# Summed neighbour layers of a graph network: steps between TensorE's results and VectorE's use of them, one PSUM bank per kind of group, inputs asked for a group ahead

## The chip, the cores and the metric

The kernel runs on one core of a Trainium2 chip. Its metric is the device time of one execution in microseconds (us); the median of three runs stands for the kernel before. TensorE (PE) does matrix products, VectorE (DVE) and ScalarE (ACT) work on elements, GpSimd (POOL) gathers rows, SyncE (SP) issues most of the transfers. L12 is line 12 of the kernel; L81, L85 and L90 lie in small helpers for VectorE's operations on two tensors, on a tensor and scalars, and on both.

## What is computed

A graph of 6250 nodes with 128 features and 100,000 edges, sorted by their target, goes through four blocks. Each block is `x = x + layer(relu(layernorm(x)))`:

```python
# block 0: mean over the incoming edges, one layer
agg = segment_sum(h[src], dst) / max(count, 1)
x = x + relu(h @ W_self.T + agg @ W_neigh.T + bias)
# block 1: a filter for each edge from its length, a product over the incoming edges
bf  = ssp(ssp(exp(coeff * (dist - centers)**2) @ W1 + b1) @ W2 + b2)
agg = segment_prod(h[src] * edge_attr * bf * cut, dst)
x = x + ssp(agg @ W3 + b3)
# block 2: three layers of the mean, relu between them
for i in range(3):
    h = relu_but_last(mean(h[src] by dst) @ W_agg[i] + h @ W_root[i] + b[i])
x = x + h
# block 3: three attention layers with batch norm
```

The change touches blocks 0 and 2, and one load of block 1.

## The kernel before

The nodes are cut into 50 tiles of 125. **A mean is formed in two ways.** For the first 38 tiles, in ten groups (`GROUPS`: nine of four tiles, one of two), it is a matrix product: an adjacency of small counts in eight-bit floats, 6250 sources by 500 targets for a group, is the moving operand, and the node rows, split into three bfloat16 parts whose sum is the float32 value, are the weights. One group takes 50 x 3 = 150 matmuls of 500 columns into one PSUM bank `o` (`product_steps`, from L1085). For the last 12 tiles, three groups of four (`LATE`), GpSimd gathers the source row of each edge, VectorE adds along the edges (195 columns in batches of five, L90), the running sums go to DRAM, and the rows at each target's last edge are fetched back; TensorE turns them (`late_sums`, from L901).

Then a group's **node terms** follow, the same for both kinds (`node_terms`, from L1097): the group's own rows, transposed, are loaded from DRAM; two matmuls make y, own rows by one matrix and the mean by the other (L1106, L1107); ScalarE adds the bias (`out_t`, L1108); TensorE turns y back (L1112); a function `rows` that the caller gives adds it to x or norms it on VectorE and ScalarE (`norm_in_two`, from L1070). All this goes through the PSUM tiles named `nt`, two of them, one bank each.

**The order is written out by hand.** These functions are generators; a `yield` marks a point at which other work may be put. Afterwards `chain` (L1149) binds every instruction of TensorE, VectorE and ScalarE to its predecessor on the same engine, so that each engine runs in just the written order. SP and GpSimd are not bound in that way, but their queues also run in order.

- *Block 0* (its `nodes_of` from L1250) still has to build the adjacencies. A step of `build_adj` (L1015) is eight one-hot rows on VectorE (L85; tiles `hot_p`, `hot_n`, three buffers each), four matmuls that count into `cnt` (L1029) and one conversion on ScalarE (L1030). A group of four has 25 steps, one of two 13. At each step stand six matmuls of the product of the group before, every second step a piece of node terms of the group before that (`follow`), and a piece of late sums (`late_`). At the end of a group's products comes the mean, `agg`, on VectorE, as the last act of `product_steps`.
- *Block 2* (`woven`, L1115; its `nodes_of` from L1319) streams the same adjacencies back from DRAM, one unit per layer and group, 30 in all. A unit has 15 slots of ten products; in slots 1, 3, 5, 7 and 9 stands a piece of node terms of the group before, in each slot a piece of late sums, and in most a piece of work for block 3 (`beside`). `Stream` (L1162) keeps `BUFS` pieces of five source tiles loaded or being loaded.
- *Block 1* (`filter_in_order`) takes blocks of sixteen columns of edges; `inputs` (L662) loads their lengths (`dist`, 1 MB, two buffers) when a block begins, and edge attributes (`ea`) and gathered rows in smaller blocks.

Of the kernel before, what the change touches and what calls it, by code (L numbers as in the profile page):

```python
# [20 lines left out]
P = 125  # L21
# [26 lines left out]
def kernel(ctx: ExitStack, tc: tile.TileContext, a: dict, out: bass.AP):  # L48
# [583 lines left out]
    def filter_in_order(table, hist, src_all, wp, pool, ps, tails):  # L632
# [28 lines left out]

        def inputs(i):  # L662
            c0 = i * HB
            if c0 % DB == 0:
                dist = pool.tile([128, DB, P], F32, name="dist", bufs=2)
                nc.sync.dma_start(dist.rearrange("p c q -> p (c q)"), bass.AP(
                    tensor=ew_dram.tensor, offset=ew_dram.offset + c0 * P, ap=[[0, 128], [1, DB * P]]))
                st["dist"] = dist
# [138 lines left out]
    def turn_rows(ht, t0, h, pool, ps):  # L807
# [3 lines left out]
        for k0, k1 in ((0, 3), (3, NW)):  # L811
            tp = ps.tile([128, 4, 128], F32, name="nt", bufs=2)
# [88 lines left out]
    def late_sums(su, table, nodes_of, pace, pool, ps):  # L901
# [9 lines left out]
        for _ in range(5):  # L911
            yield
# [18 lines left out]
        carry = ps.tile([128, NW - 1, 128], F32, name="nt", bufs=2)[:, 0, :]  # L931
# [7 lines left out]
        given = []  # L939
# [5 lines left out]
        for _ in range(4):  # L945
            yield
        for (t0, t1), rows in zip(LATE, given):
            inv = load_inv(t0, t1, pool, "_late")
            tp = ps.tile([128, NW - 1, 128], F32, name="nt", bufs=2).rearrange("f k p -> f (k p)")
            for j in range(t1 - t0):  # L950
                transpose(tp[:, j * P:(j + 1) * P], rows[:P, j, :])
            agg = pool.tile([128, NC], F32, name="agg_late", bufs=1)
            tt(agg, tp[:, :NC], inv, OP.mult)
            yield
            yield from nodes_of(t0, t1, [agg], "_late")
# [129 lines left out]
    def product_steps(parts, adj, t0, t1, agg, pool, ps):  # L1085

        n = (t1 - t0) * P
        inv = load_inv(t0, t1, pool)
# [5 lines left out]
        agg.append(pool.tile([128, NC], F32, name="agg", bufs=1))  # L1094
        tt(agg[0][:, :n], o[:, :n], inv[:, :n], OP.mult)

    def node_terms(ht, t0, t1, agg, w_agg, w_self, bias, func, rows, pool, ps, of):  # L1097
# [3 lines left out]
        own = pool.tile([128, NC], F32, name="own" + of, bufs=1)  # L1101
        nc.sync.dma_start(own[:, :n], ht[:, t0 * P:t1 * P])
        yield
        out_t = pool.tile([128, NC], F32, name="out_t" + of, bufs=1)
        y = ps.tile([128, NW - 1, 128], F32, name="nt", bufs=2).rearrange("f k p -> f (k p)")[:, :n]
        nc.tensor.matmul(y, lhsT=w_self, rhs=own[:, :n], start=True, stop=False)  # L1106
        nc.tensor.matmul(y, lhsT=w_agg, rhs=agg[0][:, :n], start=False, stop=True)  # L1107
# [7 lines left out]
    def woven(units, beside):  # L1115
# [5 lines left out]
        while ahead:  # L1121
            steps, look, then, sums = ahead
            ahead = None
            for at in range(15):
# [4 lines left out]
                if at in (1, 3, 5, 7, 9):  # L1129
                    next(follow, None)  # L1130
# [1365 lines left out]
```

## Time and profile before

| what | us |
|---|---|
| median of three runs | 5659.31 |
| lowest and highest run | 5656.65, 5667.72 |
| the profiled execution | 5665.26 |
| its span, first to last instruction | 5663.2 |

The mean clock granted to TensorE over the span is 0.863 of full speed. The shares of the span, and the stretch of each part, with what fills it:

```profile
PE 4650.4 (82%) x27333; PEld 3229.0 (57%) x27333; DVE 4038.3 (71%) x12698; ACT 3319.3 (59%) x6907; POOL 3033.6 (54%) x3016
```

| stretch, us | what |
|---|---|
| 0 to 317 | first norm, constants, index tables |
| 317 to 917 | block 0's sums |
| 930 to 2028 | block 1's filter |
| 2028 to 2207 | block 1's ends, hand-over |
| 2207 to 3263 | block 2's three layers |
| 3270 to 5663 | block 3's three attention layers |

PEld is the loading of weights, which overlaps the products. In a row of stretches the first two numbers are its bounds and its length; then come the busy time and, in brackets, the instructions of PE, PEld, DVE, ACT and POOL, the granted clock of TensorE (1.00 is full speed), the share of the 16 DMA engines and the rate in GB/s. In a row of waits stand the engine, what it was about to do with its line, after the arrow the engine and line that released it, then the total of us, how often, and the longest. Waiting costs nothing by itself; it matters on the engine that has no time to spare in that stretch.

### The profile page before, as it was taken

To read this page: it belongs to the slowest core of one execution; us is meant where nothing else is said; L and a number is where in the kernel's file an instruction comes from. 1 tells how busy PE (TensorE), PEld (TensorE's weight loads), DVE (VectorE), ACT (ScalarE), POOL (GpSimd) and SP (SyncE) were. 2 spreads that over 40 slices of the span, in tenths; PEclk is the share of its full clock that TensorE was granted. 3 is DMA by queue.
4 is the path that set the end of the run, shared out by engine and by line. 5 is a ranking of instruction groups with operands and counts; after the bars stand their busy time and mean duration, and the time that the engine had idled before them with its cause. 6 is when DMAs were issued, how large, how long until landed. Compare 5 with 4: busy or idle time off the path is not lost. (4 is left out here: it accounts for less than half of the span.)

```text
span 5663.2 us, 88527 instructions
## 1 busy us (share of the span) xinstructions
PE 4650.4 (82%) x27333; PEld 3229.0 (57%) x27333; DVE 4038.3 (71%) x12698; ACT 3319.3 (59%) x6907; POOL 3033.6 (54%) x3016
## 2 busy tenths in 40 slices
PE   3368886889888857989999959999779999599997
PEld 3224443444444433444444448888668889488886
DVE  7988773999999954766667557776377774577763
ACT  0155453999999954333333346667566668466675
POOL 0155203777777733747647347774157761377750
PEclk9999896655565568999999979999889999799998
DMA  1244324666666645889989656675466663576652
GB/s 46 51 146 148 116 81 117 194 197 198 189 197 196 190 135 153 274 289 331 321 282 327 219 188 198 193 200 154 137 175 196 195 189 96 171 200 194 197 160 83
DMA packets 574066, 1036.46 MB, mean 183 GB/s; under 512 B 113872, under 2 KB 320271, under 8 KB 571283
## 3 DMA queue, kind: packets, MB, share of 16 engines
q1 hardware_dynamic: 470888, 829.77, 45.6%
q0 software_dynamic: 96864, 198.00, 14.4%
q8 instruction: 217, 3.56, 0.3%
q10 hardware_dynamic: 5828, 2.94, 0.2%
q14 instruction: 269, 2.20, 0.1%
HBM read 690.23 MB, written 340.10 MB: 182 GB/s over the span
## 5 line engine op out<-in xcount | busy, mean ns | idle before, releaser
L63 POOL DMA_INDIRECT rows<-gtable,l_src x1200 | 1226.4, 1022 | 566.0 <-issue 328.6
L1895 PE MATMUL o<-m,hst 125*128 125x160 f32 x6000 | 943.3, 310 | 154.0 <-ACT m L2064 154.0
L1895 PEld LDWEIGHTS o<-m,hst 125*128 125x128 f32 x6000 | 902.4, 198 | 196.5 <-ACT m L2064 177.3
L63 POOL DMA_INDIRECT s_rows<-table,s_src x780 | 759.6, 974 | 429.8 <-issue 198.0
L63 POOL DMA_INDIRECT rows<-table,src_all x800 | 817.3, 1022 | 256.6 <-issue 212.7
L2059 PE MATMUL cnt<-hot_n,hot_c 128*125 128x250 f32 x3840 | 932.0, 386 | 8.0 <-ACT hot_c L1886 4.9
L1092 PEld LDWEIGHTS <-parts 128*128 128x128 bf16 x5040 | 503.6, 100 | 521.4 <-issue 57.6
L1092 PE MATMUL o<-piece,parts 128*128 128x500 fp8e4 (+1 forms) x3540 | 758.2, 373 | 7.2 <-ACT parts L1059 5.4
L2059 PEld LDWEIGHTS cnt<-hot_n,hot_c 128*125 128x125 f32 x3840 | 701.9, 192 | 84.4 <-ACT hot_c L1886 5.8
L1886 ACT ACTIVATE hot_c<-hot,coef_t 128x125 f32<-128x125 bf16 x1920 | 698.4, 389 | 0.1
L2064 ACT ACTIVATE m<-cnt 125x1000 f32<-125x1000 f32 x480 | 473.3, 986 | 29.8 <-PE cnt L2059 29.5
L693 PE MATMUL z<-w,s 128*125 128x128 f32 x1600 | 366.0, 399 | 113.4 <-DVE s L90 113.1
L90 DVE SCALAR_TENSOR_TENSOR acc<-acc,ex,rows 125x130 f32<-125x130 f32 x1197 | 424.1, 354 | 35.6
L693 PEld LDWEIGHTS z<-w,s 128*125 128x125 f32 x1600 | 313.2, 290 | 219.4 <-DVE s L90 180.3
L1030 ACT ACTIVATE adj<-cnt 128x1000 fp8e4<-128x1000 f32 x238 | 289.8, 1217 | 225.1 <-PE cnt L1029 224.6
L684 PE MATMUL z<-bf,w 128*128 128x500 f32 x400 | 369.9, 1025 | 31.4 <-ACT bf L653 27.3
L1885 ACT ACTIVATE hot_n<-half_n 128x250 f32<-128x250 bf16 x960 | 382.9, 399 | 1.9 <-DMA half_n<-node 1.6
L1092 PE MATMUL o<-adj,parts 128*128 128x500 fp8e4 (+1 forms) x1500 | 355.2, 378 | 0.0
L85 DVE TENSOR_SCALAR hot_n<-l_slot,l_id_t 128x250 f32<-128x250 f32 x960 | 301.2, 357 | 71.5 <-PE cnt L2059 47.4
L1205 ACT ACTIVATE over<-piece,few 128x1250 bf16<-128x1250 fp8e4 (+1 forms) x200 | 256.1, 1281 | 141.4 <-issue 124.7
L90 DVE SCALAR_TENSOR_TENSOR s_acc<-s_acc,s_same,s_rows 128x128 f32<-128x128 f32 x776 | 272.9, 352 | 31.1 <-DMA sum_hist<-s_acc 5.8
L653 ACT ACTIVATE soft<-soft,half 128x500 f32<-128x500 f32 (+1 forms) x400 | 286.7, 717 | 13.0
(574 smaller groups left out, 7266.8 us busy)
## 6 DMA issues: line engine op xcount, KB each, us to landing
piece<-adj SPq DMA_DIRECT2D x270, 312.5 KB
late_hist<-acc SPq DMA_DIRECT2D x150, 455.0 KB
hot<-hot SPq DMA_DIRECT2D x240, 256.0 KB
half_n<-node SPq DMA_DIRECT2D x480, 125.0 KB
dist<-ew_dram SPq DMA_DIRECT2D x50, 1000.0 KB
sum_hist<-s_acc SPq DMA_DIRECT2D x156, 320.0 KB
hot_t<-hot_t SPq DMA_DIRECT2D x192, 256.0 KB
ea<-in_edge_attr SPq DMA_DIRECT2D x100, 448.0 KB
```

The lines of the kernel that those rows point to most:

```text
L63: nc.gpsimd.indirect_dma_start(out=dst, out_offset=None, in_=table, in_offset=bass.IndirectOffsetOnAxis(ap=idx, axis=0))
L85: nc.vector.tensor_scalar(o, x, s1, None, op0=op0)
L90: nc.vector.scalar_tensor_tensor(o, x, s, y, op0=op0, op1=op1)
L684: nc.tensor.matmul(z1, lhsT=w1, rhs=bf, start=False, stop=True)
L693: nc.tensor.matmul(z2[:, j, :], lhsT=s1[:, j, :], rhs=w2, start=False, stop=j == HB - 1)
L1030: nc.scalar.activation(adj[:, :, NW * (w - w0):NW * (w - w0 + k)].rearrange("p l (w k) -> p w l k", k=NW), cnt[:, :k, :T * NW].rearrange(" ...
L1092: yield nc.tensor.matmul(o[:, :n], lhsT=parts.columns(l, 1, s)[:, 0, :], rhs=adj(l), start=(l == 0 and s == 0), stop=(l == T - 1 and s == 2))
L1885: nc.scalar.activation(hot_n[:, w, :], half_n[:, w // 2, :], AF.Copy)
L1886: nc.scalar.activation(hot_c[:, w, :P], lt.hot[:, w0 % WB + w, :P], AF.Copy, scale=coef_t[g][:, w0 + w:w0 + w + 1])
L1895: nc.tensor.matmul(o, lhsT=hst[:, l, :D], rhs=m[:P, l, :], start=(l == 0), stop=(l == T - 1))
L2059: nc.tensor.matmul(cnt[:P, w, :T * NW], lhsT=hot_c[:, w, :P], rhs=hot_n[:, w, :], start=True, stop=True)
L2064: nc.scalar.activation(m[:P, :, :, u * 4:u * 4 + 4].rearrange("p l k q -> p k l q"), cnt[:P, :, :T * NW].rearrange("p w (k l) -> p k l w", ...
```

## The change

Six things are done, all of them to the order of instructions and to buffers; the arithmetic is the same.

1. The mean is no longer taken at the end of a group's products. `product_steps` hands back a function, which `node_terms` calls as its first step, in the next group.
2. `node_terms` gets more steps: one more after y, and `gap` steps between the transposes and VectorE's use of them (four in block 0, one in block 2); ordinary groups of block 0 begin four steps later. In exchange a piece is taken at every step in block 0, not at every second, and in nine slots of a unit in block 2, not in five.
3. `late_sums` waits `lead` steps ahead of the first batch (eight in block 0; ten, five, five in block 2; it was five), seven steps in place of four ahead of the late groups, and `gap` between their transposes and the mean.
4. The two `nt` banks become one `nt` for ordinary groups and one `nt_late` for late ones.
5. Own rows are loaded by `load_own` as soon as a group's products begin (for late groups a group ahead), into two buffers.
6. In block 1 the lengths of a block are asked for one block ahead, into three buffers; `BUFS` goes from 12 to 11.

```diff
@@ -659,13 +659,18 @@
             act(l, l, AF.Ln, bias=half[:o.shape[0]], scale=0.5)
             stt(o, z, 0.0, l, OP.max, OP.add)
 
+        def distances(c0):
+            dist = pool.tile([128, DB, P], F32, name="dist", bufs=3)
+            nc.sync.dma_start(dist.rearrange("p c q -> p (c q)"), bass.AP(
+                tensor=ew_dram.tensor, offset=ew_dram.offset + c0 * P, ap=[[0, 128], [1, DB * P]]))
+            return dist
+
         def inputs(i):
             c0 = i * HB
             if c0 % DB == 0:
-                dist = pool.tile([128, DB, P], F32, name="dist", bufs=2)
-                nc.sync.dma_start(dist.rearrange("p c q -> p (c q)"), bass.AP(
-                    tensor=ew_dram.tensor, offset=ew_dram.offset + c0 * P, ap=[[0, 128], [1, DB * P]]))
-                st["dist"] = dist
+                st["dist"] = st.pop("dist_ahead", None) or distances(c0)
+                if c0 + DB < C:
+                    st["dist_ahead"] = distances(c0 + DB)
             if c0 % NB == 0:
                 rows = pool.tile([128, NB, D], F32, name="rows", bufs=4)
                 ea = pool.tile([P, NB, D], F32, name="ea", bufs=4)
@@ -808,8 +813,8 @@
 
         on_pe = []
         h_t = pool.tile([128, NW, P], F32, name="h_turned", bufs=1)
-        for k0, k1 in ((0, 3), (3, NW)):
-            tp = ps.tile([128, 4, 128], F32, name="nt", bufs=2)
+        for k0, k1, of in ((0, 3, ""), (3, NW, "_late")):
+            tp = ps.tile([128, 4, 128], F32, name="nt" + of, bufs=1)
             on_pe += [nc.tensor.transpose(tp[:, k - k0, :P], h[:, k, :], ident[:P, :P]) for k in range(k0, k1)]
             nc.scalar.activation(h_t[:, k0:k1, :], tp[:, :k1 - k0, :P], AF.Copy)
         nc.sync.dma_start(ht[:, t0 * P:(t0 + NW) * P], h_t.rearrange("f k p -> f (k p)"))
@@ -898,7 +903,13 @@
 
     SB = 5
 
-    def late_sums(su, table, nodes_of, pace, pool, ps):
+    def load_own(ht, t0, t1, pool, of=""):
+        own = pool.tile([128, NC], F32, name="own" + of)
+        nc.sync.dma_start(own[:, :(t1 - t0) * P], ht[:, t0 * P:t1 * P])
+        return own
+
+    def late_sums(su, table, ht, nodes_of, pool, ps, lead, pace, gap):
+
 
 
         def rows_of(c0):
@@ -908,7 +919,7 @@
             return rows
 
         given, prev = [rows_of(0), rows_of(SB)], None
-        for _ in range(5):
+        for _ in range(lead):
             yield
         for b, c0 in enumerate(range(0, C3, SB)):
             if c0 + 2 * SB < C3:
@@ -928,7 +939,7 @@
         fixed = pool.tile([128, D], F32, name="s_fixed", bufs=1)
         nc.gpsimd.memset(fixed, 0.0)
         gather_some(fixed, sum_hist, su.fix, 128 * C3)
-        carry = ps.tile([128, NW - 1, 128], F32, name="nt", bufs=2)[:, 0, :]
+        carry = ps.tile([128, NW - 1, 128], F32, name="nt_late", bufs=1)[:, 0, :]
         nc.tensor.matmul(carry, lhsT=su.flow, rhs=prev, start=True, stop=True)
         held = pool.tile([128, D], F32, name="s_held", bufs=1)
         nc.scalar.activation(held, carry, AF.Copy)
@@ -936,23 +947,27 @@
             yield
         tt(fixed, held, fixed, OP.add)
         scatter(sum_hist, su.fix, fixed, 128 * C3)
-        given = []
+        given, own = [], [None, load_own(ht, *LATE[0], pool, "_late")]
         for t0, t1 in LATE:
             rows = pool.tile([128, SB, D], F32, name="s_rows", bufs=4)
             for j in range(t1 - t0):
                 gather(rows[:, j, :], sum_hist, su.end[:, t0 - TE + j:t0 - TE + j + 1])
             given.append(rows)
-        for _ in range(4):
+        for _ in range(7):
             yield
         for (t0, t1), rows in zip(LATE, given):
-            inv = load_inv(t0, t1, pool, "_late")
-            tp = ps.tile([128, NW - 1, 128], F32, name="nt", bufs=2).rearrange("f k p -> f (k p)")
+            own, inv = own[1:], load_inv(t0, t1, pool, "_late")
+            if t1 < T:
+                own.append(load_own(ht, t1, t1 + 4, pool, "_late"))
+            tp = ps.tile([128, NW - 1, 128], F32, name="nt_late", bufs=1).rearrange("f k p -> f (k p)")
             for j in range(t1 - t0):
                 transpose(tp[:, j * P:(j + 1) * P], rows[:P, j, :])
+            for _ in range(gap):
+                yield
             agg = pool.tile([128, NC], F32, name="agg_late", bufs=1)
             tt(agg, tp[:, :NC], inv, OP.mult)
             yield
-            yield from nodes_of(t0, t1, [agg], "_late")
+            yield from nodes_of(t0, t1, [own[0], lambda agg=agg: agg], "_late")
 
 
 
@@ -1082,34 +1097,43 @@
             ts(h[:, j, :], x[:, j, :], mv[:, j, 0:1], OP.subtract, rstd[:, j:j + 1], OP.mult)
         nc.scalar.activation(h, h, AF.Relu)
 
-    def product_steps(parts, adj, t0, t1, agg, pool, ps):
+    def product_steps(parts, adj, ht, t0, t1, agg, pool, ps):
 
         n = (t1 - t0) * P
+        agg.append(load_own(ht, t0, t1, pool))
         inv = load_inv(t0, t1, pool)
         o = ps.tile([128, NC], F32, name="o", bufs=2)
         for l in range(T):
             for s in range(3):
                 yield nc.tensor.matmul(o[:, :n], lhsT=parts.columns(l, 1, s)[:, 0, :], rhs=adj(l),
                                        start=(l == 0 and s == 0), stop=(l == T - 1 and s == 2))
-        agg.append(pool.tile([128, NC], F32, name="agg", bufs=1))
-        tt(agg[0][:, :n], o[:, :n], inv[:, :n], OP.mult)
-
-    def node_terms(ht, t0, t1, agg, w_agg, w_self, bias, func, rows, pool, ps, of):
+
+        def mean():
+            m = pool.tile([128, NC], F32, name="agg", bufs=1)
+            tt(m[:, :n], o[:, :n], inv[:, :n], OP.mult)
+            return m
+
+        agg.append(mean)
+
+    def node_terms(t0, t1, agg, w_agg, w_self, bias, func, rows, pool, ps, of, gap):
 
 
         n = (t1 - t0) * P
-        own = pool.tile([128, NC], F32, name="own" + of, bufs=1)
-        nc.sync.dma_start(own[:, :n], ht[:, t0 * P:t1 * P])
+        own, mean = agg
+        mean = mean()
         yield
         out_t = pool.tile([128, NC], F32, name="out_t" + of, bufs=1)
-        y = ps.tile([128, NW - 1, 128], F32, name="nt", bufs=2).rearrange("f k p -> f (k p)")[:, :n]
+        y = ps.tile([128, NW - 1, 128], F32, name="nt" + of, bufs=1).rearrange("f k p -> f (k p)")[:, :n]
         nc.tensor.matmul(y, lhsT=w_self, rhs=own[:, :n], start=True, stop=False)
-        nc.tensor.matmul(y, lhsT=w_agg, rhs=agg[0][:, :n], start=False, stop=True)
+        nc.tensor.matmul(y, lhsT=w_agg, rhs=mean[:, :n], start=False, stop=True)
         nc.scalar.activation(out_t[:, :n], y, func, bias=bias, scale=1.0)
         yield
-        r = ps.tile([128, NW - 1, 128], F32, name="nt", bufs=2)[:P, :t1 - t0, :]
+        yield
+        r = ps.tile([128, NW - 1, 128], F32, name="nt" + of, bufs=1)[:P, :t1 - t0, :]
         for k in range(t1 - t0):
             nc.tensor.transpose(r[:, k, :], out_t[:, k * P:(k + 1) * P], ident)
+        for _ in range(gap):
+            yield
         rows(r, out_t[:, :n])
 
     def woven(units, beside):
@@ -1126,7 +1150,7 @@
                     pass
                 if at == 0:
                     ahead = next(units, None)
-                if at in (1, 3, 5, 7, 9):
+                if at in (0, 1, 2, 3, 4, 5, 6, 8, 9):
                     next(follow, None)
                 if sums and at == (10 if late else 0):
                     for _ in late or ():
@@ -1163,7 +1187,7 @@
 
 
 
-        L, BUFS = 5, 12
+        L, BUFS = 5, 11
 
         def __init__(self, pool):
             self.pool, self.tiles, self.at, self.seen = pool, {}, -1, 0
@@ -1253,7 +1277,10 @@
                     def rows(y, _):
                         stt(x, y, 0.0, x, OP.max, OP.add)
 
-                    yield from node_terms(ht_dram[0], t0, t1, agg, w_n, w_s, bias, AF.Identity, rows, pool, ps, of)
+                    if not of:
+                        for _ in range(4):
+                            yield
+                    yield from node_terms(t0, t1, agg, w_n, w_s, bias, AF.Identity, rows, pool, ps, of, 4)
                     bulk(turned(x_after[0], t0, t1 - t0), x)
                     h_n = pool.tile([P, NW - 1, D], F32, name="h_n" + of, bufs=1)[:, :t1 - t0, :]
                     yield from norm_in_two(h_n, x, t1 - t0)
@@ -1263,7 +1290,7 @@
 
                 traced = nc.cur_bb.bb.instructions
                 n0 = len(traced)
-                late_ = late_sums(su, table[0], nodes_of, 3.6, pool, ps)
+                late_ = late_sums(su, table[0], ht_dram[0], nodes_of, pool, ps, 8, 3.6, 4)
                 before, follow, then = iter(()), iter(()), iter(())
                 for t0, t1 in GROUPS:
                     n = (t1 - t0) * P
@@ -1271,14 +1298,13 @@
                     for step, _ in enumerate(build_adj(t0, t1, flat, pool, ps, hi_t, id_t, slots_b)):
                         for _ in islice(before, 6 if t1 - t0 == 4 else 12):
                             pass
-                        if step % 2:
-                            next(follow, None)
+                        next(follow, None)
                         next(late_, None)
                     for piece in (before, follow):
                         for _ in piece:
                             pass
                     agg = []
-                    before = product_steps(parts, lambda l, flat=flat, n=n: flat[:, l * n:(l + 1) * n], t0, t1, agg, pool, ps)
+                    before = product_steps(parts, lambda l, flat=flat, n=n: flat[:, l * n:(l + 1) * n], ht_dram[0], t0, t1, agg, pool, ps)
                     follow, then = then, nodes_of(t0, t1, agg)
                 for piece in (before, follow, then, late_):
                     for _ in piece:
@@ -1326,18 +1352,19 @@
                         nc.sync.dma_start(ht_dram[2 + i][:, t0 * P:t1 * P], y_t)
                         split(parts[i + 1], t0, n, h, pool)
 
-                    yield from node_terms(ht_dram[1 + i], t0, t1, agg, w_a[i], w_r[i], bias[i], AF.Relu, rows, pool, ps, of)
+                    yield from node_terms(t0, t1, agg, w_a[i], w_r[i], bias[i], AF.Relu, rows, pool, ps, of, 1)
                     yield
                     return
                 x = pool.tile([P, NW - 1, D], F32, name="h_g" + of, bufs=1)[:, :n, :]
                 bulk(x, turned(x_after[1], t0, n))
-                yield from node_terms(ht_dram[3], t0, t1, agg, w_a[i], w_r[i], bias[i], AF.Identity, lambda y, _: tt(
-                    x, y, x, OP.add), pool, ps, of)
+                yield from node_terms(t0, t1, agg, w_a[i], w_r[i], bias[i], AF.Identity, lambda y, _: tt(
+                    x, y, x, OP.add), pool, ps, of, 1)
                 bulk(turned(x_dram, t0, n), x)
                 h = pool.tile([P, NW - 1, D], F32, name="h_g3" + of, bufs=1)[:, :n, :]
                 yield from norm_in_two(h, x, n)
                 yield
-                tp = ps.tile([128, NW - 1, 128], F32, name="nt", bufs=2).rearrange("f k p -> f (k p)")[:, :n * P]
+                yield
+                tp = ps.tile([128, NW - 1, 128], F32, name="nt" + of, bufs=1).rearrange("f k p -> f (k p)")[:, :n * P]
                 for k in range(n):
                     nc.tensor.transpose(tp[:, k * P:(k + 1) * P], h[:, k, :], ident[:P, :P])
                 p0, p1 = t0 * P // T, t1 * P // T
@@ -1349,7 +1376,7 @@
                 for i in range(3):
                     for g, (t0, t1) in enumerate(GROUPS):
                         agg = []
-                        steps = product_steps(parts[i], adj.unit(i * len(GROUPS) + g), t0, t1, agg, pool, ps)
+                        steps = product_steps(parts[i], adj.unit(i * len(GROUPS) + g), ht_dram[1 + i], t0, t1, agg, pool, ps)
                         if i == g == 0:
 
                             with tc.tile_pool(name="r1tw", bufs=1) as nw, tc.tile_pool(name="r1t", bufs=2) as np_, \
@@ -1363,7 +1390,8 @@
                                 in_turn(steps)
                         late_ = None
                         if i == 0 and g == 1 or i and g == 0:
-                            late_ = late_sums(su, table[2 + i], lambda *args, i=i: nodes_of(i, *args), 2.8, pool, ps)
+                            late_ = late_sums(su, table[2 + i], ht_dram[1 + i], lambda *args, i=i: nodes_of(i, *args),
+                                              pool, ps, 5 if i else 10, 2.8, 1)
                         yield steps, adj.look, lambda args=(i, t0, t1, agg): nodes_of(*args), late_
 
             def beside():
```

## The prediction

> **What bounds the kernel now.** I read the page's first two parts, then its chain of waits. The chain cannot serve here: it is followed back only to about 3191 us, and all that the change touches lies before. So I cut the span by the source lines in the timeline: the first layer's sums (317–917 us), the filter (930–2028), the three later sum layers (2207–3263), attention (3270 to the end; no line of it changes). Then the busy time of each engine by stretch:
>
> ```profile
> core 0: us, PE busy (x) PEld busy (x) DVE busy (x) ACT busy (x) POOL busy (x), PEclk, DMA share, GB/s
> 317.00:917.00 600.00, 511.53 (x2566) 264.53 (x2566) 461.51 (x2283) 307.06 (x276) 201.81 (x211) 0.94 0.35 117
> 817.00:842.00 25.00, 25.00 (x149) 14.35 (x148) 20.69 (x113) 18.27 (x15) 0.00 (x0) 1.00 0.01 2
> 342.00:367.00 25.00, 18.22 (x54) 5.46 (x55) 24.57 (x124) 14.94 (x13) 19.05 (x22) 1.00 0.35 103
> 2207.00:3263.00 1056.00, 994.11 (x4766) 493.06 (x4767) 673.42 (x2576) 351.47 (x536) 605.42 (x624) 0.96 0.86 284
> ```
>
> To be seen: in the first layer no engine is full (PE idle 88 us, DVE 138), yet a late stretch (817) has PE at 25.00 of 25 and an early one (342) DVE at 24.57. Two engines each have all the work in turn, and between lie stretches in which they wait for each other. The later layers are TensorE's: idle 62 of 1056 us. So next the waits, first layer first, then the later layers:
>
> ```profile
> DVE x_sb L90 <- PE nt L1112: 59.9, 12, 12.0
> DVE agg L81 <- PE o L1092: 32.5, 9, 9.1
> DVE agg L81 <- PE nt L1107: 17.1, 1, 17.1
> DVE agg_late L81 <- PE nt L168: 12.1, 3, 5.5
> PE cnt L1029 <- DVE hot_n L85: 61.0, 30, 4.7
> ```
>
> ```profile
> PE nt L1106 <- DMA own<-ht: 15.9, 2, 10.2
> PE nt L168 <- DMA s_rows<-sum_hist,s_end: 15.6, 7, 9.7
> PE nt L1342 <- ACT h_g_late L1083: 10.7, 3, 4.7
> ```
>
> The first four say that VectorE stands 122 us (59.9 + 32.5 + 17.1 + 12.1) for TensorE, about 5 us a time; the fifth is the answer to it: TensorE then has no one-hot rows. Both engines run in written order, and VectorE may be only three steps ahead (three buffers of one-hots), so each such stop empties the pipe twice. In the later layers 42 of 62 idle us are in those three rows.
>
> **First layer.** Between writes of finished adjacencies the groups take 49.3, 49.9 (no node terms yet), 59.6, 59.1, 59.1, 57.2, 88.6 (all three late groups), 52.0, 51.7, 46.9 us, then 16 us of bare products and 13 of node terms. The change removes no instruction; it moves the mean behind the next group's first steps, lets a step or more pass between the y product, its transposes and VectorE's sum, and spreads the late groups over more steps. TensorE's count rises by 29 of 35,652 entries: nothing. After it VectorE's own work is the floor: 49.9 us of one-hots and late sums, plus about 4 of node terms per group (mean 0.67, sum 0.69, statistics about 1.7, the rest about 1): 53.5–54.
> - Groups 2 to 5: 235 us become 4 × 53.5–54, −20.
> - Group 6: 36 of one-hots (8 × 0.18 × 25), 4 of node terms, 12 of late groups, or TensorE's 42: 88.6 becomes about 52, −36.
> - Groups 7 to 9: the 817 stretch runs 149 matmuls in 25 us, so a step's ten take 1.68 and 25 steps 42 us; with node terms 45.5–49: −3, −6, −5.
> - The serial end: the mean of group 9 now stands on VectorE after the node terms of group 8, which puts off its y product: +4 to +5.
>
> Sum −65, taken as −62. From one side, −25 if only half of the stops go and what is gained comes back as one-hot waits; from the other −75: the idle PE is 88 us, and the bare products and node terms at the end (some 16) stay.
>
> Does a step suffice? In the order of TensorE's instructions y stands at step 5 of a group, the transposes at 7, VectorE's sum four steps later. VectorE is at most three steps ahead, so TensorE is past the transposes when it asks. The added distance queues nothing: one-hots stand behind it.
>
> **PSUM.** Two shared buffers become one for ordinary and one for late groups. Here the Trainium skill speaks against the change (Perfetto Trace Analysis, Matmuls): independent groups should rotate through banks, so that emptying one overlaps the next. By the rule, y and its transposes in one bank wait for ScalarE's read; each of 40 ordinary and 12 late groups would pay one eviction (ScalarE's L1108, 0.68 us): +35. The rows say otherwise: the transposes read what ScalarE makes of y, so they wait for it with any number of banks (only `PE nt L1112 <- ACT out_t` 5.3 us for two, in the first layer), and the next group's y comes ten or more steps later. By the row 0; I take 0. A gain is possible (a late group no longer takes the ordinary one's bank), and is in the rows above.
>
> **Later layers.** Own rows are asked for a group (32 us) ahead instead of one slot. The timeline shows the stop:
>
> ```profile
> 2797.01 2.03 PE L1106 MATMUL nt<-own,w_r 128*128 128x500 f32 x2 [10.20 <-DMA own<-ht]
> ```
>
> and another of 5.7; with 32 us lead both go, −16. Longer waits before the late groups (7 slots for 4, lead 10 for 5 in the first layer) put about 90 products, 20 us, before the first late transpose, where the fetch needed 23: of 15.6 some 12 go. The waits for ScalarE and VectorE (the row of 10.7, and 5.4, 5.1, 4.7 and 3.6 below it) get a slot of 2 us or two: about 20 of 29 go. Together −48 of the idle 62.
>
> The clock adds. After the 5.13 us stop at 2326 the products run at 0.42 us each, against sixteen in 3.54 us (0.22) at 2447. The skill (TensorE: Matmul & The Clock Gate, Part 1) gives half speed for a window of 3.4 us after an idle stretch of such length; that makes 1.7 us a stop, six stops: −10. By the mean granted clock of 0.96 it would be up to −38. I take −12, since the row's slow run is about 4 us, 2 lost a stop; other dips have short causes that stay.
>
> Against that: counted in slots along the order of instructions, the late sums of the third layer now need about 153 and have 139. So the last 14 slots, a whole late group (transposes, mean, y, transposes, norm, transposes: 11 to 13 us) run after the last product with nothing beside, at half clock, ahead of attention. Now 7.4 us pass there (3262.5 to 3269.9); then 20 to 24: +15. The first layer needs 149 of 145, so four slots are flushed, +2; the second fits. One buffer less of streamed pieces (11 for 12) leaves 11 × 3.2 = 35 us ahead: 0, and if that cover went, the stream's wait would be at most its 3 us a time. SP: a group's load of inverse counts waits for the previous mean, now four steps later in the first layer (8 us), and the own load and one or two stores of late sums queue behind it; these have two buffers and a pitch of 3.6 steps: 0, at worst 8 us × 6. In the later layers it waits one slot, 2 us, under the 35 of pieces.
>
> Sum −48 − 12 + 15 + 2 = −43, taken −40; from −60 (everything but half the tail's price) to 0.
>
> **Filter.** VectorE and ScalarE are busy 984 and 979 of 1098 us, and the gathers on POOL keep a pitch of 1.25 us × 800 throughout; ScalarE waits for distances once, 9.1 us, at the start. So asking a block ahead has nothing to remove. But SP now issues two loads of 1 MB before the first edge attributes, for which VectorE waits 16.2 us at the start. 1 MB at the stage's 190 GB/s is 5 us; part runs beside. +3, from 0 to +6.
>
> **Sum.** −62 − 40 + 3 = −99 on a profiled execution of 5665.3 (span 5663.2): 5566. The profile is 6 us above the median of 5659.3; against the median 5560.
>
> **Rivals.**
> - *The later layers give nothing* (0.20). Their DMA share is 0.86, 1.0 in long stretches; if the stops only gave the streams time to catch up, TensorE then waits for pieces. For: the own load landed late in such a stretch. Against: at 2557–2782 the share is about 1 and PE full; 0.86 × 1056 is 908 us of DMA, 100 under what I forecast. B −62, rest +3: 5600.
> - *VectorE bounds the whole first layer* (0.08): groups 6 to 9 keep their times, −20 + 5, with −40 + 3: 5607. Against: the 817 stretch, DVE 20.69 of 25.
> - *The steps change nothing that is waited for* (0.05), as the queues' real distance is unlike the written one: 5655. Against: order is enforced on TensorE, VectorE and ScalarE.
> - *Slower: late groups laid bare at layer changes* (0.07). Their gathers come 23 us after the sums and three groups make 36 us; before, about 20 of the 59 were paid. If spreading pushes them past the point where the next layer's products need their rows, each of two changes and the end shows 40 us more: +120. With −62, −20 of other stops, +3: 5700. It decides from 27 us a hand-over on. Against: the count of slots flushed (4, 0, 14).
>
> **Numbers.** Likeliest 0.60 at 5560, its own range 5525–5595. About 0.2% (11 us) is what a measurement tells from no change. Faster is the likeliest, the first two rivals: 0.88, less a little since the third lies near the bound; same 0.05, slower 0.07. The range 5515–5635 takes in the first two rivals.
>
> **What would show it.** The first layer's stretch should be about 538 us with DVE's waits for `nt` and `o` under 25 in place of 122, and group 6 near 52; no `own<-ht` wait on TensorE; clock in the later layers 0.98; from the last product to `y L1748` 20 to 24 us; the filter's first wait for edge attributes up to 5 longer. It would be wrong if PE waits for pieces, if one-hot waits on TensorE stay at 61, or if the hand-overs grow.

## The result and the profile after

The changed kernel takes 5566.09 us (median of four runs, 5557.58 to 5567.29), where the kernel before now has 5663.40 (four runs, 5656.65 to 5667.72). The ratio is 0.9826, its interval 0.9809 to 0.9843, so 89 to 108 us less. The forecast was 5560. The profiled execution of after is the fastest of the four, 5557.58 us (span 5555.7), 8.5 under the median; the spans differ by 107.5.

The span is cut again at points that both programs have: the transpose ahead of block 0's sums (L168, `fs_row`), the first gather of the filter, block 2's first product, the end of its last, and the first y product of attention.

| stretch | before | after | change |
|---|---|---|---|
| block 0's sums, to the filter's first gather | 614.9 | 538.2 | -76.7 |
| filter and hand-over, to block 2's first product | 1142.9 | 1143.7 | +0.8 |
| block 2's products | 1191.1 | 1149.6 | -41.5 |
| last product to attention's first y product | 7.0 | 26.0 | +19.0 |
| attention | 2393.3 | 2383.9 | -9.4 |

With 0.3 before the first point this makes -107.5. The attention code is the same; in three kernels below that leave it alone too (`both`, `nt_shared`, `b_nogap`) it took 2386.6, 2391.7 and 2399.8 us. So its -9.4 is within the spread from run to run, and is about what the profiled execution lies below its median.

Block 0 first: the busy times by stretch of the profile after (columns as before the prediction).

```profile
317.00:840.00 523.00, 482.41 (x2566) 257.67 (x2566) 460.34 (x2280) 306.50 (x276) 202.53 (x211) 0.99 0.41 134
2131.00:3147.00 1016.00, 978.23 (x4746) 483.86 (x4744) 666.74 (x2548) 346.40 (x529) 605.74 (x624) 0.98 0.89 295
3147.00:3171.80 24.80, 8.46 (x25) 4.30 (x24) 9.69 (x37) 6.60 (x11) 0.00 (x0) 0.68 0.16 44
```

In the first row the same 2566 matmuls keep TensorE busy 482 us in place of 512: the granted clock is 0.99 where it was 0.94. The other 48 us of the gain are idle time of TensorE, 88 before and 41 now. VectorE's waits in block 0, and the answer to them on TensorE:

```profile
PE cnt L1044 <- DVE hot_n L85: 20.6, 19, 3.2
...
DVE x_sb L90 <- PE nt L1134: 18.6, 1, 18.6
...
DVE agg L81 <- PE o L1108: 1.3, 1, 1.3
```

Of VectorE's 122 us of stops for TensorE 20 are left. The twelve for `nt` (59.9 us) became one, 18.6 us at the serial end, where before the mean stood 17.1 us; the 32.5 for `o` became 1.3. TensorE's 61.0 for one-hots fell to 20.6. In the other direction VectorE now reaches the end of its three one-hot buffers more often: it waits for TensorE's counts 18.8 us, in place of 5.9. The lengths of the groups (numbered from 0) come from the rows in which SP stores each adjacency; five of the ten, from the timeline of SP:

```profile
573.30 0.32 SPq L1048 DMA_DIRECT2D adj<-adj  x1
...
625.56 0.32 SPq L1048 DMA_DIRECT2D adj<-adj  x1
...
675.22 0.34 SPq L1048 DMA_DIRECT2D adj<-adj  x1
...
728.91 0.34 SPq L1048 DMA_DIRECT2D adj<-adj  x1
...
774.49 0.34 SPq L1048 DMA_DIRECT2D adj<-adj  x1
```

So groups 5 to 8 take 52.3, 49.7, 53.7 and 45.6 us; before they took 57.2, 88.6, 52.0 and 51.7.

In block 2 TensorE's waits are no longer those of before. First the row of before for the mean, which the forecast did not show, and VectorE's for a load of the side work; then the profile after, 2131 to 3171 us:

```profile
PE nt L1107 <- DVE agg L81: 5.1, 1, 5.1
DVE ee_hot_t L85 <- DMA ee_rows<-part: 66.2, 26, 5.5
```

```profile
DVE ee_hot_t L85 <- DMA ee_rows<-part: 72.4, 33, 6.5
PE nt L1128 <- DVE agg L81: 23.4, 10, 6.2
PE nt_late L1369 <- ACT h_g_late L1098: 12.1, 3, 4.9
PE nt_late L168 <- DMA s_rows<-sum_hist,s_end: 6.4, 2, 5.5
PE nt L1369 <- ACT h_g L1098: 5.9, 4, 3.1
```

`own<-ht` (15.9) is gone and `s_rows` fell from 15.6 to 6.4; the 12.1 for `h_g_late` has 8.7 of the end in it, told below. But the wait for the mean, 5.1 before, is now 23.4 in ten stops, while VectorE's own wait for `ee_rows` has hardly grown. TensorE waits for no piece of the stream. The largest stop, on SP, VectorE and TensorE in the timeline:

```profile
2728.20 0.32 SPq L1676 DMA_DIRECT2D ee_rows<-part  x1
...
2735.22 0.49 DVE L85 TENSOR_SCALAR ee_hot_t<-ee_rows,ee_here 128x1024 bf16<-128x1024 bf16 x1 [6.45 <-DMA ee_rows<-part]
...
2735.98 1.90 DVE L90 SCALAR_TENSOR_TENSOR s_acc<-s_acc,s_same,s_rows 128x128 f32<-128x128 f32 x5
2737.80 0.67 DVE L81 TENSOR_TENSOR agg<-o,inv 128x500 f32<-128x500 f32 x1
...
2738.53 2.04 PE L1128 MATMUL nt<-agg,w_a 128*128 128x500 f32 x2 [6.17 <-DVE agg L81]
```

A load of 256 KB for the side work (`ee_rows`), asked for at 2728.2, lets VectorE start only at 2735.2. The sums and the mean stand behind it in VectorE's written order, and TensorE waits 6.17 us for the mean. The row names VectorE as releaser, but the late one is a transfer. Ahead of each of the other nine stops, too, VectorE waits for a transfer within the 8 us before, in seven of them for `ee_rows`.

And the end of block 2, from the timeline of TensorE in the profile after:

```profile
3141.78 1.00 PE L1127 MATMUL nt_late<-own_late,w_r 128*128 128x500 f32 x2
...
3143.46 2.31 PE L1108 MATMUL o<-piece,parts 128*128 128x250 fp8e4 x20
3145.61 0.60 PE L1134 MATMUL nt_late<-ident,out_t_late 128*125 128x128 f32 x4
3146.05 0.59 PE L1127 MATMUL nt<-own,w_r 128*128 128x250 f32 x2
...
3157.70 1.09 PE L168 MATMUL nt_late<-ident,s_rows 125*128 125x125 f32 x4 [1.21 <-ACT y_t L1371]
3159.57 2.03 PE L1127 MATMUL nt_late<-own_late,w_r 128*128 128x500 f32 x2 [0.77 <-DVE agg_late L81]
...
3169.52 1.09 PE L1369 MATMUL nt_late<-ident,h_g_late 125*128 125x125 f32 x4 [4.92 <-ACT h_g_late L1098]
3171.83 2.53 PE L1776 MATMUL y<-l_w_ext,y_t 128*125 128x130 f32 x10 [1.21 <-ACT y_t L1371]
```

A whole late group, from the turning of its rows to its last transposes, runs alone after the last product. The two matmuls of L1127 take 2.03 us there; the same pair between products takes 1.00 (the row at 3141.78). The granted clock of these 25 us is 0.68, as the third row of the stretches says.

### The profile page after: what moved, and what is told of

Same layout as the page of the kernel before. It is cut to its first block, busy times and chain, and to the rows that moved or that the text cites. A ratio compares the mean times of both kernels' runs of the same rounds, so it can differ in the third digit from the quotient of the medians.

```text
span 5555.7 us, 88517 instructions
## 1 busy us (share of the span) xinstructions
PE 4607.8 (83%) x27333; PEld 3210.3 (58%) x27333; DVE 4039.5 (73%) x12698; ACT 3319.5 (60%) x6907; POOL 3036.2 (55%) x3016
## 4 chain that ended last, share of the span: by engine, by line
PE 21%; DVE 10%; DMA 9%; ACT 6%; POOL 5%; issue 4%; SPq 0%; DVEq 0%; ACTq 0%; POOLq 0%
PE o L1923 8%; PE cnt L2087 5%; POOL rows L63 5%; PE o L1108 4%; DMA rows<-gtable,l_src 2%; DVE acc L90 2%; DMA ee_rows<-part 2%; ACT hot_c L1914 2%; ACT m L2092 1%; DMA hot_n<-first 1%; PE x_ps L1846 1%; DMA sum_hist<-s_acc 1%; PE at_ps L2025 1%; ACT hot_n L1913 1%; DVE hot_n L85 1%
## 5 line engine op out<-in xcount | busy, mean ns | idle before, releaser
L1108 PE MATMUL o<-adj,parts 128*128 128x500 fp8e4 (+1 forms) x1500 | 339.4, 366 | 0.0
L90 DVE SCALAR_TENSOR_TENSOR s_acc<-s_acc,s_same,s_rows 128x128 f32<-128x128 f32 x776 | 272.9, 352 | 50.4 <-DMA sum_hist<-s_acc 19.3
```

The source lines that it names most:

```text
L90: nc.vector.scalar_tensor_tensor(o, x, s, y, op0=op0, op1=op1)
L1108: yield nc.tensor.matmul(o[:, :n], lhsT=parts.columns(l, 1, s)[:, 0, :], rhs=adj(l), start=(l == 0 and s == 0), stop=(l == T - 1 and s == 2))
```

## The experiments

Each kernel below is timed against the kernel before on its own chip; in brackets behind a time stand its ratio to that of before and the 95% interval. Three of the four comparisons fell on chips on which every kernel, the one before too, takes about 7060 us, because all engines stand for up to some 20 us at a time with a releaser that the profile calls "remote" or "issue"; there only kernels of one such chip, or the same stretch, are compared. The other one, with `b_nogap`, `nt_shared` and `both`, was on a chip where before takes 5655.99.

**Block 0 without its distance.** `b_nogap`, where before takes 5655.99:

```diff
-                    yield from node_terms(t0, t1, agg, w_n, w_s, bias, AF.Identity, rows, pool, ps, of, 4)
+                    yield from node_terms(t0, t1, agg, w_n, w_s, bias, AF.Identity, rows, pool, ps, of, 4 if of else 0)
```

> The kernel after, but in block 0 VectorE's sum of an ordinary group stands right behind TensorE's transposes (no four steps between them). Theory: VectorE, up to three steps ahead, stops again for nt, about 3 to 5 us for each of ten groups, and TensorE then for one-hots: block 0 is 25 to 40 us longer than after. Rival: where VectorE is the bound it is not ahead and hardly waits, and the rest of the rearrangement did the work: at most 10 us longer.

It takes 5598.65 us (0.9892, 0.9875 to 0.9908). Block 0 is 567.8 us long, 29.6 more than in after. Its waits:

```profile
DVE x_sb L90 <- PE nt L1134: 60.9, 9, 18.6
...
PE cnt L1044 <- DVE hot_n L85: 36.1, 20, 3.1
```

VectorE's stops for `nt` are back: 42.3 us in eight, beside the 18.6 of the serial end, which after has too. TensorE's for one-hots come with them. Of the 29.6 us, 14 are slower matmuls: the same 2570 of this stretch take 498 us at a granted clock of 0.95, where after has 484 at 0.98. The theory holds and the rival falls: four steps between transposes and sum are worth some 30 of the 77 us. What stays is telling too: groups 6 and 7, which hold the late groups, take 111.4 us together, 103.4 in after and 140.5 before. So some 29 us of the gain there come without these four steps of the ordinary groups; the wider spacing of the late groups is the likely cause, but no run takes it out alone.

**The place of the mean.** `b_mean_now` (before: 7077.89):

```diff
-        agg.append(mean)
+        m = mean() if now else None
+        agg.append((lambda: m) if now else mean)
```

with `now` set in block 0 alone.

> The kernel after, but in block 0 the mean stands on VectorE at the end of its group's products, as before the change, and not in the next group's fifth step. Theory: VectorE stops there for o, about 3 to 4 us for each of nine groups, and the pipe of one-hots empties with it: block 0 is 15 to 35 us longer than after. Rival: the four steps between transposes and sum are what counts, the mean's place is worth under 8 us.

Block 0 takes 647.5 us; in three other kernels of that chip whose block 0 is that of after, 635.9, 637.7 and 639.0. VectorE waits for `o` 44.1 us, nine times, in place of 1.3. So the later mean is worth 8.5 to 11.6 us, under the theory's 15 and little over the rival's 8; with one profile of each kernel, and 3 us between the three alike, it is a rough figure. Most of the 44 us does not show in the length of the block; where it is made up was not traced. The whole time (0.9939, 0.9922 to 0.9955) can't be told from that of the others.

**One bank each, or two shared.** `nt_shared` (before: 5655.99):

```diff
-        y = ps.tile([128, NW - 1, 128], F32, name="nt" + of, bufs=1).rearrange("f k p -> f (k p)")[:, :n]
+        y = ps.tile([128, NW - 1, 128], F32, name="nt", bufs=2).rearrange("f k p -> f (k p)")[:, :n]
```

and likewise for every other tile of that name.

> The kernel after, with the two kinds of groups sharing two buffers named nt, as before, in place of one bank each. The rule of rotating banks would make this faster (a group's transposes do not share a bank with its y): by up to 35 us over 52 groups. The recorded forecast says 0: the transposes wait for ScalarE's reading of y with any number of banks; a late group that holds one of the two while it waits its steps may cost up to 10 us in block 0's groups 6 and 7.

5564.87 us (0.9833, 0.9816 to 0.9849); block 0's stretch is 537.9 us against 538.2, and VectorE's wait for `nt` is 18.6 us, once, as in after. The banks are worth nothing that can be measured here. This kernel serves below as another after, on the chip of `both`.

**Each block's part alone.** `block0_only` and `block2_only` (before: 7048.04) hold the functions of both kernels side by side; one block calls the new ones, the other the old. In essence:

```diff
-                late_ = late_sums(su, table[0], nodes_of, 3.6, pool, ps)
+                late_ = late_sums_n(su, table[0], ht_dram[0], nodes_of, pool, ps, 8, 3.6, 4)
```

> The kernel before, with the change made in block 0 alone (own functions for it; blocks 1 and 2 as before). Theory: the gain of block 0 stands by itself, the first gather of the filter comes 76 us sooner, and later stretches keep their lengths: about 5587 where before takes 5663. Rival: part of the 107 us between the two profiled spans comes in attention as a consequence of block 0 or 2; then attention (from the first y product to the end) is again 9 us shorter than 2393 here.

> The kernel after, with blocks 0 and 1 as before the change. Theory: block 2 gains 40 us from its first products to the last and gives 18 back between the last product and attention, so about 20 us in all: 5643 where before takes 5663. Rival: the recorded forecast for block 2, 40 us net: 5623. If attention is 9 us shorter here too, that belongs to block 2's change and not to the spread of runs.

Block 0 alone: 7005.10 us (0.9933, 0.9913 to 0.9952). Block 2 alone: 7068.95 us, slower than before (1.0023, 1.0005 to 1.0040). Block 0's stretch takes 633.5 us in `block0_only`, with the new order, and 685.3 in `block2_only`, with the old: the gain stands by itself here too, 52 us in place of 77. From first product to attention `block0_only`, with the old order in block 2, takes 1456.1 us, `block2_only` with the new one 1496.2. The expected 5587 and 5643 can't be judged on this chip, nor can the length of attention. What the pair does show is a sign: where engines stand more often, the new order of block 2 loses. Its cause is not shown; TensorE's stops with the releaser "issue" among the products, 173 us against 150, are more than half of the 40. Two of its named waits:

```profile
PE nt L1189 <- ACT out_t L1184: 22.7, 2, 15.7
...
PE nt L1183 <- DVE agg L81: 18.9, 4, 13.2
```

**The end of block 2.** `packed` takes 18 slots out of the third layer's late groups:

```diff
-                                              pool, ps, 5 if i else 10, 2.8, 1)
+                                              pool, ps, (10, 5, 2)[i], 2.8, int(i < 2), 7 if i < 2 else 4)
```

with one `yield` less before a late group's transposes, its last transposes and its sum.

> The kernel after, but in the third layer of block 2 the late sums begin three slots sooner and the late groups have the narrow spacing of before (three slots less ahead of them, none of the extra steps inside), 18 slots less in all; so no late group is left behind the last product. Theory: the 26 us between the last product and attention's first y product fall to about 10, and the late groups' stops on TensorE among the products grow by at most 8: 8 to 16 us faster than after. Rival: the narrow spacing brings back at least what the end gives, so within 4 us of after.

> The same kernel as packed (third layer's late groups with the spacing of before), looked at again since the first look was on a chip on which every kernel took a quarter longer. From the run both: the end falls from 26 to 7 us and about 6 come back among the products: 12 us faster than after.

7001.83 us (0.9938, 0.9913 to 0.9962; before 7048.04) and 7029.10 (0.9931, 0.9906 to 0.9956; before 7077.89). After itself was not run on these chips, so the whole time says little; the end does: from the last product's start to attention 7.0 us in both, where five kernels of those chips with the spacing of after have 26.5 to 27.1.

**A slot more for the mean.** `y_later`:

```diff
+        for _ in range(0 if of else late_y):
+            yield
```

between the mean and the y product, with slot 7 added to those of `follow`.

> The kernel after, with one more slot between the mean and the y product of ordinary groups in block 2 (VectorE gets about 4.4 us where it has 2.2). Theory: TensorE's 23 us of waits for agg (ten times) are VectorE being a few us late behind other work in its written order; most of them go, and 15 to 20 us of block 2 with them. Rival: VectorE is short of time as such, the wait moves to the transposes and to later steps (h_g, h_g_late), and the time stays within 5 us of after.

> The same kernel as y_later (one more slot between mean and y in block 2), looked at again for the same reason. Theory as at first: 15 to 20 us faster than after. Rival, which the run both speaks for: the waits for agg halve, others take their place, and the time is within 4 us of after.

6961.52 us (0.9889, 0.9863 to 0.9914) and 6999.12 (0.9862, 0.9813 to 0.9912): 40 and 30 us under `packed` on the same chips. TensorE's waits for `agg` in block 2 are gone in the first and 1.4 us, once, in the second; in `packed` and `packed_b` they are 11.5 and 23.7. So on these chips `y_later` is ahead by more than was expected, though it keeps the long end that `packed` removes. It is also more than the waits for `agg` come to, so they can't be the whole of it, and the intervals of the second pair overlap. After itself was not run here.

**Both edits**, where before takes 5655.99:

> The kernel after with both edits of the runs y_later and packed: one more slot between mean and y in block 2's ordinary groups, and the narrow spacing for the third layer's late groups. Theory: the two do not touch each other; from the last product to attention about 7 us in place of 26, and TensorE's waits for agg in block 2 under 8 us in place of 23: about 30 us faster than after, 130 faster than before. Rival: the late groups' stops among the products take back what the end gives: 15 us faster than after.

5554.31 us (0.9823, 0.9806 to 0.9839), against 5564.87 of `nt_shared` on that chip: 10.6 less, nearer the rival's 15 than the theory's 30, and the two intervals overlap. Its end is 7.0 us long, so 19 were to be had; but the products take 1155.4 us, against 1149.6, 1152.3 and 1154.6 in after, `nt_shared` and `b_nogap`. The wait for `agg` halved to 12.6 us, and no shorter products came of it. That is what the rival of `y_later` says, but the narrow spacing stands in the same kernel, and `y_later` alone was not run on this chip. Ahead of five of the six stops for `agg` that are left stands a wait of VectorE for `ee_rows`, within 8 us:

```profile
DVE ee_hot_t L85 <- DMA ee_rows<-part: 90.7, 37, 6.1
```

It is 72.4 us in after and 90.7 here. A possible reading is that VectorE comes sooner and waits longer for the same transfers.

**That load asked for two steps ahead.** `rows_ahead` is `both` with

```diff
-                    if w0 + WB < 128:
-                        rows = rows_of(g, w0 + WB)
+                    if w0 + 2 * WB < 128:
+                        rows.append(rows_of(g, w0 + 2 * WB))
```

> The kernel both, with one more edit in block 2's side work: each 256 KB load of ee_rows is asked for two steps ahead and not one (the same two buffers). In the profile after, VectorE waits 72 us for these loads (33 times, up to 6.5), and ahead of seven of the eight listed stops of TensorE for agg stands such a wait, or one for another transfer, in VectorE's written order. Theory: the stops for agg are transfers that land late on full DMA queues, passed on by VectorE; with more lead VectorE's wait for ee_rows falls under 25 us, TensorE's for agg under 5, and the kernel is 5 to 15 us faster than both (about 1.9 to 2.0 percent faster than before). Rival: the DMA engines are full, so the lead of one transfer is the lateness of another (pieces, s_rows, sums): the waits change names and the time stays within 4 us of both.

6997.57 us (0.9877, 0.9849 to 0.9906; before 7076.98). In block 2 VectorE waits for `ee_rows` nowhere, and TensorE's waits for `agg` are one of 3.8 us. That looks like the cause, but it is no proof: on chips of this kind the slot of `y_later` had already done as much while VectorE still waited for the load. The rows of `y_later_b`:

```profile
PE nt L1130 <- DVE agg L81: 1.4, 1, 1.4
...
DVE ee_hot_t L85 <- DMA ee_rows<-part: 44.7, 16, 10.6
```

The time can't be told from that of the two runs of `y_later` either, and it fell on a chip other than that of `both`. So the run shows that a longer lead removes VectorE's waits for this load; what TensorE gains by it, and whether the kernel is faster where before takes 5660, stays open.

**Own rows asked for late.** `own_short` (before: 7077.89):

```diff
+            if ask and l == ask:
+                agg.append(load_own(ht, t0, t1, pool))
```

with `ask` = 46 of 50 source tiles, in block 2 alone.

> The kernel after, but in block 2 the ordinary groups' own rows are asked for twelve products ahead of the group's end (about 2 slots, 5 us before use, as before the change) and not a group ahead. Forecast's step: two or three such loads come late behind full DMA queues, TensorE waits for own again, 10 to 16 us in all, and the time grows by as much. Rival: VectorE's mean for the same y product is late too in this order, so the load is hidden behind it: under 4 us.

7031.16 us (0.9937, 0.9915 to 0.9960), the same as its neighbours; TensorE waits for `own` once, 3.7 us, and 9.6 for `agg`. On that chip the rival holds, under 4 us; that the load is hidden behind a late mean fits the two waits and was not tested apart. Where before takes 5660, this kernel was not run.

## Why the prediction was right, and where its terms were off

The time, the range and the order of the parts held: 5560 forecast, 5566 measured, block 0 the larger part. That the sum came so near is partly luck: block 0 gave 15 us more than was taken, block 2 about 17 less. The forecast's 538 us for block 0's stretch is no hit either: it is measured from 600, which became 523; the 538.2 of the table has other bounds (614.9 before).

- **VectorE's stops in block 0** were the cause, as said. -62 was taken, -76.7 came. Groups 2 to 5: -23.5 for -20; group 6: -38.9 for -36; group 7: +1.7 for -3, since the late groups now reach into it; 8 and 9: -6.1 and -8.3 for -6 and -5; the serial end +1.0 for +4 to +5. The first two groups, expected at 0, gave -2.6. The sum of the terms had been -65, and rounding it to -62 had no ground; the rest is in these differences. For group 9 the forecast had a wrong floor: it counted 25 steps of 1.68 us, but this group has two tiles and 13 steps (with twelve products each), and came out at 38.6 us, with TensorE busy throughout.
- **"A step suffices"** (VectorE at most three steps ahead) held: one stop for `nt` is left, at the serial end.
- **PSUM at 0** held: `nt_shared` differs in block 0 by 0.3 us. The rule of rotating banks (the Trainium skill, Perfetto Trace Analysis, Matmuls) speaks of independent groups of matmuls; y and its transposes are not, since the transposes read what ScalarE makes of y. So the +35 that the forecast drew from it was not what the page promises.
- **Block 2's idle time, -48 of 62, is the term that failed**: 62 became 38, -24. Own rows gave their 16 and `s_rows` 9 of 12. The step that failed was that waits for ScalarE and VectorE "get a slot of 2 us or two: about 20 of 29 go". Up to 3147 us four of these five rows fell from 24.4 to 6.7 us, but the wait for the mean grew from 5.1 to 23.4, and nothing was gained. Overlooked was that the change shortens this one distance: before, the mean stood on VectorE at the end of a group's products and y in slot 3 of the next group; now the mean is in slot 0 and y in slot 1, ten products between them in place of 40. In the timelines, y follows the mean within 0.2 us in 2 of the 30 groups before and in 14 after. VectorE's lateness, mostly for transfers, was there before (66.2 us for `ee_rows`); it no longer has the slots to hide in. This account is read from the traces. A slot more halved the wait (`both`) or ended it (`y_later`), which agrees, but where before takes 5660 no shorter products came of it.
- **The clock in block 2**: -12 taken; TensorE's busy time fell by 16 (994 to 978), clock 0.96 to 0.98. Of these 16 some 4 are 20 matmuls that now stand behind the window, in the end (an estimate, at the mean of 0.21 us of 994 in 4766). That leaves 12, as taken.
- **The flushed end**: +15 taken, +19.0 came, and 26 us pass where 20 to 24 were forecast. The count of slots (14 too few) fits, and `packed` and `both`, with 18 slots less, have that end at 7 us again. The group alone took longer than 11 to 13 us, from its row at 3157.70 to 3171.83, about 14; and ahead of it group 9 and another late group had to end.
- **Block 2 in all**: -40 taken, -22.5 measured in these two profiles (-41.5 and +19.0).
- **SP and the late sums, 0**: VectorE's wait for the store of its sums grew from 5.8 us to 19.3 in thirteen stops. The longest, 4.36 us at 2369.1, had its store issued at 2362.2, so it seems to have landed late; it was not held in SP behind a load of counts, as had been feared. What it adds to the mean's lateness was not measured by itself.
- **The filter, +3**: +0.8. The first edge attributes came sooner, not later (VectorE waits 1.3 us for them, not 16.2; the first product of the z matmuls 10.7 us after the first gather, not 18.3), and nothing came of that: the stretch is as long as before.

## What to carry to other kernels

When two engines run in a fixed order and each may be only a few steps ahead, put a consumer's instruction further behind its producer's than that lead: of 77 us in block 0, about 30 hang on four such steps and, by runs on another chip, about 10 on the place of one operation. And see that no other distance gets shorter by the same edit: here ten products instead of 40 stand between the mean and its use, and TensorE's wait for it grew from 5 to 23 us. Distance is paid for in slots, so count them to the end of the stage: what no longer fits runs alone (19 us here). Where a wait names an engine, look what that engine waited for: ahead of the longest stop for a mean, 6.17 us, VectorE stood 6.45 us for a side load of 256 KB that it got 7 us after it was asked for.

## What the runs showed that was not expected

Short stops cost more than their length: the same 2566 matmuls took 512 us of TensorE at a granted clock of 0.94 and 482 at 0.99, so 29 of 77 us came as faster matmuls; `b_nogap` brought half of its stops' cost back in that way. And the worth of a distance depends on the chip: the new order of block 2 gained 22 us between two profiles where before takes 5660, and cost 0.23% (0.05 to 0.40) on a chip on which engines stand more often. One slot more for the mean put the kernel 30 to 40 us ahead of `packed` on such chips, while on the first, beside the narrow spacing, it gave nothing that could be measured. What makes those chips stand was not found.
